# Steps of lead in a hand-scheduled attention loop: an even rate for the projections, one more empty piece ahead of some products, and maxima that end one step sooner

## The chip, the cores and the metric

The kernel runs on one core of a Trainium2 chip. The core has five engines that run side by side: TensorE (PE in the profile, with its weight loads as PEld), VectorE (DVE), ScalarE (ACT), GpSimd (POOL) and SyncE (SP), which issues most of the DMA. The metric is device time in microseconds (us); the number of a kernel is the median of its runs.

## What is computed

One transformer block with adaptive layer norm: causal attention with rotary position encoding, then a mixture of experts of which each token takes four of sixteen. There are 4 batches of 2048 tokens, 256 channels, 16 heads of 16 channels each. Cut to the part around the change:

```python
h = _layernorm(x) * (1 + ca) + sa
qkv = (h @ qkv_w + qkv_b)            # q, k: rotary
scores = einsum('bhqd,bhkd->bhqk', q, k) * scale   # causal mask
attn = softmax(scores)
x = x + ga * ((attn @ v) @ out_w + out_b)
h = _layernorm(x) * (1 + cb) + sb
x = x + gb * moe(h)                  # routing: top 4 of 16 experts, in 2 of 4 groups
```

## The kernel before, in words

Tokens are cut into 16 blocks of 512 (`NB`), four to a batch. The kernel has two stages: attention up to about 2780 us of the profiled execution, then the experts. The change lies in attention alone, though `send`, which carries a block over to the experts, is called in both stages.

**The main loop (L1204 to L1283).** A unit is one or two pairs of a block `n` and a group `g` of four heads: 16 units of one pair for batch 0, then 8 units of two pairs for each of the other batches, 40 in all (`units`, L927). A unit's steps go over its key tiles of 128: block `n` of a batch has 4 x (n % 4 + 1) of them, so that batch 0 makes 160 steps, each other batch 160, 640 in all. In a step TensorE puts the row maxima (product with `pick`, L1240) and the scores (L1247) into two PSUM tiles `st`, ScalarE takes exponentials into `e` (L1255), GpSimd masks the diagonal tiles (L1259), and one step later `weigh` (L1181) multiplies by the values into `po` (L1188). Of the last four key tiles of a block only 512, 384, 256 and 128 columns are computed.

**Maxima.** While a unit runs, the row maxima of the next one are made: `row_max` (L956) is a generator of pieces. Each computes scores into a PSUM tile `ps` (L968, from the same three buffers as `st`) that VectorE reduces (L978, L1001). Its last piece joins the parts into `negm` and splits them into three bf16 parts `mb` (L1014 to L1025). Then `max_rows` (L1028), after one empty piece, transposes `mb` on TensorE (`pmx`, L1034), and ScalarE copies the result to `mt`, which the next unit's first step needs. `draw` (L1219) spreads the pieces over the steps in proportion to `share` (L1211): 2 for a full step, less for a shortened one, with the last two steps left out. Two calls of `draw` in each step pull at most two pieces each.

**Background pieces.** Everything else in attention is a generator too, kept in one of six queues (`Background`, L65). A generator yields what its next piece needs: (a PSUM piece or not, VectorE time, GpSimd time). The `Budget` (L43) grants one PSUM piece for each step, since all of these products share one PSUM buffer (`wps`, one `"w"` tile), and a running account of VectorE and GpSimd time. `(0, 0, 0)` is an empty piece: it issues nothing and is there to put what follows later in the order. At a step's end (L1276 to L1282) the queues are served in turn: `over` (one piece, division by the row sum), `after_max` (one), `ends` (two, `finish`: output projection), `ahead` (projections), `after` (three: `send` and others).

**Projections (`prologue`, L814).** There are twelve, for the blocks of batches 1 to 3: load x, layer norm (`normalise`, L230), transposes (`pt`), then for each of four tiles of 128 tokens the products `pq` (L866) and `pv` (L879), rotary products on GpSimd (L893, L902), a transpose `ptq` (L907) of the rotated rows, copies on ScalarE and stores to DRAM. One is 48 pieces (`PIECES`, L922). How fast they are drawn is set by `marks` (L1168): for each unit that needs more projections than the one before, the step at which its loads are issued and the number of projections it needs. `due` (L1175) goes in straight lines between marks; a queue more than 8 pieces behind is pulled by force (L1279), else pieces are pulled as the budget allows, up to the due count.

**Send (`send`, L342).** For a block of the first twelve: load, layer norm, modulation on GpSimd, transposes, routing products (`lg`, L384), the ranks of `route` (L266: VectorE and GpSimd in turn), a count of the positions (`pk`, L402), and 16 scatters. Its argument `apart` is the number of empty pieces between an operation and one that takes its result on another engine: 1 in attention, 3 in the experts' stage. `normalise` has an argument `apart` of the same sense, 1 when the projections call it.

TensorE, ScalarE, VectorE and GpSimd run in the order in which the code issues (a manual schedule): a product whose input is late holds up all that stand behind it on TensorE.

Of the kernel before, what the change touches and what calls it, by code (L numbers as in the profile page):

```python
# [21 lines left out]
BT = 512  # L22
# [101 lines left out]
def adaln_attention_moe(  # L124
# [105 lines left out]
    def normalise(xb, pools, xn, apart=1):  # L230

        mv = pools.tile([P, 4, 2], F32, tag="mv", name="mv")
        for t in range(4):
            yield 0, 0.6, 0
            st = pools.tile([P, 6], F32, tag="bst", name="bst")
            nc.vector.bn_stats(st, xb[:, t, :])
            nc.vector.bn_aggr(mv[:, t, :], st)
        yield 0, 0.2, 1.0
        rs = pools.tile([P, 4], F32, tag="rs", name="rs")
        nc.vector.tensor_scalar_add(rs, mv[:, :, 1], EPS)  # L240
        nc.gpsimd.tensor_tensor(rs, rs, mhalf, ALU.pow)  # L241
        for _ in range(apart):
            yield 0, 0, 0
        for t in range(4):
            if t % 2 == 0:
                yield 0, 0.9, 0
            nc.vector.tensor_scalar(
                xn[:, t, :], xb[:, t, :], mv[:, t, 0:1], rs[:, t : t + 1], ALU.subtract, ALU.mult
            )
        return xn  # L250
# [320 lines left out]
    with ExitStack() as actx:  # L571
        acst = actx.enter_context(tc.tile_pool(name="acst", bufs=1))
        kvp = actx.enter_context(tc.tile_pool(name="kv", bufs=3))
        xp = actx.enter_context(tc.tile_pool(name="xa", bufs=1))
        tp = actx.enter_context(tc.tile_pool(name="ta", bufs=2))
# [4 lines left out]
        wps = actx.enter_context(tc.tile_pool(name="wps", bufs=1, space=PSUM))  # L580
# [233 lines left out]
        def prologue(n):  # L814

            b, qb = divmod(n, NQ)
            yield 0, 0, 0
            xb = xp.tile([P, 4, D], F32, tag="xp", name="xb")
            nc.sync.dma_start(xb, x[n * BT : (n + 1) * BT, :].rearrange("(t p) d -> p t d", p=P))
            for _ in range(3):  # L820
                yield 0, 0, 0
            xn = yield from normalise(xb, tp, xb)
            yield 1, 0, 0

            def evict(to, pt, k):
                nc.scalar.activation(
                    to,
                    pt,
                    AF.Identity,
                    bias=mod[:, k, b : b + 1],  # L830
                    scale=mod[:, 2 + k, b : b + 1],
                )

            hT = yield from transposed(xn, "hT", tp, wps, "w", evict)


            rest = None
            parts_ = [None]

            def high_low(t, pt):  # L840

                if t % 2 == 0:
                    parts_[0] = tuple(
                        tp.tile([P, 4, HB], FR, tag=name, name=name, bufs=1)
                        for name in ("high", "low")
                    )
                cols = slice(t % 2 * P, (t % 2 + 1) * P)
                nc.scalar.copy(parts_[0][0][:, :, cols], pt)
                whole = tp.tile([P, 4, P], F32, tag="whole", name="whole", bufs=1)
                nc.scalar.copy(whole, pt)  # L850
                return cols, whole

            def lower(cols, whole, high, low):
                nc.gpsimd.tensor_tensor(
                    low[:, :, cols], whole, high[:, :, cols].bitcast(F32), ALU.subtract
                )

            def halved(half, high, low):
                store(n, slice(half * HB, (half + 1) * HB), high, low, (nc.sync, nc.sync))

            for t in range(4):
                lT = [hT[:, k, t * P : (t + 1) * P] for k in range(2)]
                yield 1, 0.7, 0
                pq = wps.tile([P, BT], F32, tag="w", name="pq")
                for k in range(2):
                    nc.tensor.matmul(  # L866
                        pq, lhsT=lT[k], rhs=wqkv[:, k, : 2 * D], start=(k == 0), stop=(k == 1)
                    )
                qk = tp.tile([P, 2 * D], F32, tag="qk", name="qk", bufs=1)
                nc.vector.tensor_add(qk, pq, bqkv[:, : 2 * D])  # L870
                yield 0, 0, 1.3 if rest is not None else 0
                if rest is not None:
                    lower(*rest)
                    if t == 2:
                        halved(0, *rest[2:])
                yield 1, 0.4, 0
                pv = wps.tile([P, D], F32, tag="w", name="pv")
                for k in range(2):
                    nc.tensor.matmul(  # L879
                        pv, lhsT=lT[k], rhs=wqkv[:, k, 2 * D :], start=(k == 0), stop=(k == 1)  # L880
                    )
                nc.vector.tensor_add(
                    vh[:, :, t, :, 1:],
                    pv.rearrange("p (g h e) -> p g h e", g=NG, e=HD),
                    bqkv[:, 2 * D :].rearrange("p (g h e) -> p g h e", g=NG, e=HD),
                )
                parts = qk.rearrange("p (h e two) -> p h e two", e=HD // 2, two=2)
                full = [P, 2 * H, 2, HD // 2]
                prod = []
                for s in range(2):  # L890
                    yield 0, 0, 1.3
                    r_ = tp.tile(full, F32, tag=f"r{s}", name=f"r{s}", bufs=1)
                    nc.gpsimd.tensor_tensor(  # L893
                        r_,
                        parts[:, :, :, s].unsqueeze(2).to_broadcast(full),
                        rp[:, qb * 4 + t, s].unsqueeze(1).to_broadcast(full),
                        ALU.mult,
                    )
                    prod.append(r_.rearrange("p h a e -> p h (a e)"))
                xr = prod[0]  # L900
                yield 0, 0, 1.3
                nc.gpsimd.tensor_tensor(xr, xr, prod[1], ALU.add)  # L902
                yield 0, 0, 0
                yield 1, 0, 0
                pt = wps.tile([P, 4, P], F32, tag="w", name="ptq")
                for c_ in range(4):
                    nc.tensor.transpose(  # L907
                        pt[:, c_, :],
                        xr[:, 8 * c_ : 8 * c_ + 8, :].rearrange("p h d -> p (h d)"),
                        ident,  # L910
                    )
                cols, whole = high_low(t, pt)
                high, low = parts_[0]
                rest = (cols, whole, high, low)
            yield 0, 0, 1.3
            lower(*rest)
            yield 0, 0, 0
            halved(1, *rest[2:])
            nc.sync.dma_start(vd[n], va_new)


        PIECES = 48  # L922
        qts, kts, vas = {}, {}, {}


# [102 lines left out]
        def max_rows(n, g, mb):  # L1028

            yield 0, 0, 0  # L1030
            yield 1, 0, 0
            pm = wps.tile([P, 2, BT], BF, tag="w", name="pmx")
            for t in range(4):
                nc.tensor.transpose(pm[:, 0, t * P : (t + 1) * P], mb[:, t, :], idb)  # L1034
            mt = tp.tile([P, BT], BF, tag="mt", name="mt", bufs=3)
            nc.scalar.copy(mt, pm[:, 0, :])
            mts[n, g] = mt
# [31 lines left out]
        def finish(n):  # L1069
# [15 lines left out]
            xb = xp.tile([P, 4, D], F32, tag="xf", name="xb")  # L1085
# [27 lines left out]
                nc.vector.tensor_add(xb[:, halves[t2]], xb[:, halves[t2]], ps)  # L1113
            nc.sync.dma_start(x1d[n], xb.rearrange("p t d -> p (t d)"))
            if phase_of[n] is phases[0]:
                after.add(send(n, xp, tp, wps, "w"))
                finished.append(n)
                if len(finished) == len(phases[0].blocks):
                    after.add(find_tiles(phases[0]))

        budget = Budget()
        ahead, maxes, after_max, over, ends, after = (Background(budget) for _ in range(6))
# [38 lines left out]
        need, starts = [], [0]  # L1161
# [6 lines left out]
        marks = [(0, 0)]  # L1168
        for u in range(len(units)):

            step = starts[u - 1] - (starts[u - 1] - starts[u - 2]) // 3 if u > 1 else 0
            if need[u] > marks[-1][1]:
                marks.append((step, need[u]))

        def due(at):  # L1175
            for (a0, v0), (a1, v1) in zip(marks, marks[1:]):
                if at <= a1:
                    return int(-(-PIECES * (v0 + (v1 - v0) * (at - a0) / (a1 - a0)) // 1))
            return PIECES * marks[-1][1]

# [23 lines left out]
        for u, unit in enumerate(units):  # L1204
            steps_ = []
            for n, g in unit:
# [1 line left out]
                steps_ += [  # L1208
                    (n, g, k_, first_ + 4, max(0, k_ - first_) * P) for k_ in range(first_ + 4)
                ]  # L1210
            share = [2.0 - st_[4] / BT for st_ in steps_[: len(steps_) - 2]]  # L1211
            left = 0
            if u + 1 < len(units):
                left = max_pieces(units[u + 1])
# [75 lines left out]
    xp = ctx.enter_context(tc.tile_pool(name="xm", bufs=2))  # L1290
    tp = ctx.enter_context(tc.tile_pool(name="tm", bufs=2))
# [419 lines left out]
```

## Time and profile before

| | us |
|---|---|
| median of 3 runs | 3854.46 |
| lowest, highest | 3839.63, 3859.56 |
| the profiled execution | 3858.31 |
| its span, first to last instruction | 3856.1 |

| engine | busy us | share of the span | instructions |
|---|---|---|---|
| TensorE | 3230.1 | 84% | 19884 |
| VectorE | 2547.2 | 66% | 4534 |
| ScalarE | 1506.2 | 39% | 2140 |
| GpSimd | 1467.9 | 38% | 2170 |

The profile's page cuts the span into 40 slices of 96.4 us and gives each engine's busy share in tenths, with a row for the clock that TensorE was granted. A group is one line of the kernel on one engine: busy time and mean duration, then the engine's idle time just ahead of it, and what released it. A wait is named by the instruction that waited, then the one that it waited for. TensorE's busy time is modelled: its matmuls overlap. The mean granted clock over the span is 0.894.

### The profile page before, as it was taken

The numbers are of one execution on the slowest core, as the hardware profiler recorded it, in microseconds if no ns is written. First come the engines' busy times: TensorE is split into PE (matmuls) and PEld (weight loads), VectorE is DVE, ScalarE is ACT, GpSimd is POOL, SyncE is SP. The second block draws the span as 40 slices with busy tenths as digits, with TensorE's granted clock in tenths as the row PEclk, the third lists the DMA queues.
The fourth block names the chain that finished last, engine by engine and source line by source line (L and its number), as shares of the span: only waits on it lengthen the run. The fifth ranks groups of instructions, "written<-read, shape, count | busy, mean of one in ns | idle before, by whom it ended". The sixth has DMA issues, their size and how long they took to land. (4 is left out here: it accounts for less than half of the span.)

```text
span 3856.1 us, 55123 instructions
## 1 busy us (share of the span) xinstructions
PE 3230.1 (84%) x19884; PEld 1672.2 (43%) x20008; DVE 2547.2 (66%) x4534; ACT 1506.2 (39%) x2140; POOL 1467.9 (38%) x2170
## 2 busy tenths in 40 slices
PE   5388888888899989888898888899888898798893
PEld 3233333333334333333433333343366676575562
DVE  5256767766767767677767777677266576567774
ACT  1134444444454544444454444455522222121120
POOL 3213251522414253433425334311135555445554
PEclk8569988989899988988999999899988898899997
DMA  4444232321233322233333222311086666587763
GB/s 153 157 142 156 99 120 81 121 93 58 84 115 109 113 87 89 91 106 107 115 108 99 85 95 93 98 62 41 27 286 229 214 227 228 195 278 263 263 232 132
DMA packets 264635, 525.80 MB, mean 136 GB/s; under 512 B 26014, under 2 KB 133534, under 8 KB 264354
## 3 DMA queue, kind: packets, MB, share of 16 engines
q1 hardware_dynamic: 233890, 440.37, 33.6%
q0 software_dynamic: 26112, 73.44, 5.1%
q10 hardware_dynamic: 4352, 8.39, 0.6%
q8 instruction: 159, 2.61, 0.3%
q14 instruction: 122, 1.00, 0.1%
HBM read 336.47 MB, written 185.62 MB: 135 GB/s over the span
## 5 line engine op out<-in xcount | busy, mean ns | idle before, releaser
L1255 ACT ACTIVATE e<-st 128x1024 f32<-128x1024 f32 (+3 forms) x1280 | 1078.7, 895 | 1035.1 <-PE st L1247 978.7
L978 DVE TENSOR_REDUCE mparts<-ps 128x2 f32<-128x1024 f32 (+3 forms) x1152 | 1180.7, 1045 | 429.2 <-PE ps L968 367.1
L968 PE MATMUL ps<-kt,qt 64*128 64x512 f32 (+3 forms) x3328 | 619.5, 418 | 132.9 <-ACT e L1255 64.7
L1188 PE MATMUL po<-e,vg 128*32 128x512 f32 (+3 forms) x5120 | 671.7, 590 | 24.6 <-POOL e L1259 15.4
L968 PEld LDWEIGHTS ps<-kt,qt 64*128 64x128 f32 x3328 | 305.7, 205 | 730.9 <-ACT e L1255 443.4
L1259 POOL TENSOR_SCALAR_AFFINE_SELECT e<-e 128x256 f32<-128x256 f32 x512 | 206.8, 414 | 961.9 <-ACT e L1255 957.8
L1247 PE MATMUL st<-qt,kt 64*128 64x512 f32 (+3 forms) x2560 | 462.0, 441 | 0.0
L1358 PE MATMUL gu<-xT,wt 128*128 128x256 f32 x1728 | 416.5, 397 | 14.4 <-DVE xT L1347 8.3
L1461 POOL DMA_INDIRECT yd<-yt,to x288 | 282.8, 982 | 334.2 <-ACT yt L1457 140.3
L1240 PE MATMUL st<-mt,pick 32*128 32x512 bf16 (+3 forms) x2560 | 302.6, 372 | 94.8 <-DVE mparts L978 51.0
L1358 PEld LDWEIGHTS gu<-xT,wt 128*128 128x128 f32 x1728 | 333.4, 197 | 93.9 <-issue 36.2
L453 POOL DMA_INDIRECT xs<-row,rowx x256 | 249.0, 973 | 212.2 <-DVE row L444 157.4
L1001 DVE TENSOR_REDUCE mparts<-ps 128x8 f32<-128x1024 f32 x128 | 156.8, 1225 | 187.2 <-PE ps L968 170.3
L1247 PEld LDWEIGHTS st<-qt,kt 64*128 64x128 f32 x2560 | 205.3, 198 | 137.8 <-issue 125.9
L1240 PEld LDWEIGHTS <-pick 32*128 32x128 bf16 x2560 | 87.9, 91 | 311.1 <-issue 297.9
L1457 ACT ACTIVATE yt<-y,of 128x256 f32<-128x256 f32 x144 | 60.5, 471 | 396.5 <-DVE is L1437 140.9
L1188 PEld LDWEIGHTS po<-e,vg 128*32 128x32 f32 x5120 | 109.2, 112 | 182.9 <-issue 122.2
L1396 PE MATMUL y<-wt,ha 128*128 128x256 f32 x576 | 152.8, 404 | 30.5 <-issue 27.1
L893 POOL TENSOR_TENSOR r<-qk,rp 128x512 f32<-128x512 f32 x96 | 124.0, 1307 | 96.4 <-DVE qk L870 96.4
L241 POOL TENSOR_TENSOR rs<-rs,mhalf 128x4 f32<-128x4 f32 x32 | 34.9, 1090 | 265.1 <-DVE rs L240 209.1
L1396 PEld LDWEIGHTS y<-wt,ha 128*128 128x128 f32 x576 | 110.9, 202 | 55.1 <-issue 38.5
L1370 DVE TENSOR_TENSOR hb<-hb,gu 64x256 f32<-64x256 f32 x144 | 59.3, 412 | 105.6 <-ACT hb L1369 79.7
(227 smaller groups left out, 3639.8 us busy)
## 6 DMA issues: line engine op xcount, KB each, us to landing
wt<-in_w_all SPq DMA_DIRECT2D x144, 640.0 KB
kt<-kd SPq DMA_DIRECT2D x124, 512.0 KB
xt<-xs SPq DMA_DIRECT2D x144, 272.0 KB
qt<-qd SPq DMA_DIRECT2D x64, 512.0 KB
yg<-yd SPq DMA_DIRECT2D x16, 2048.0 KB
vg<-vd SPq DMA_DIRECT2D x124, 168.0 KB
xb<-in_x SPq DMA_DIRECT2D x32, 512.0 KB
qd<-high SPq DMA_DIRECT2D x96, 128.0 KB
```

What stands on the lines that cost most here:

```text
L453: s_ = nc.gpsimd.indirect_dma_start(out=ph.xs[:, :], out_offset=bass.IndirectOffsetOnAxis(ap=rowx[:, n, t, j : j + 1], axis=0), in_=row[:, ...
L968: nc.tensor.matmul(ps[:, half, to : to + width], lhsT=qt[rows, q, t * P : (t + 1) * P], rhs=kt[rows, q, key : key + width], start=start, s ...
L978: nc.vector.tensor_reduce(to, ps[:, :, :width], AX.X, ALU.max)
L1001: nc.vector.tensor_reduce(mine[:, :, :, 0], ps.rearrange("p h (t k) -> p h t k", k=P), AX.X, ALU.max,)
L1188: nc.tensor.matmul(po[32 * j : 32 * j + 32, off:], lhsT=va[:, k_, j * (HD + 1) : j * (HD + 1) + 32], rhs=es[j // 2][:, j % 2, off:], start ...
L1240: nc.tensor.matmul(sts[q][:, h_, off:], lhsT=pick[rows, :], rhs=mt[rows, off:], start=True, stop=False,)
L1247: nc.tensor.matmul(sts[q][:, h_, off:], lhsT=kt[rows, q, k_ * P : (k_ + 1) * P], rhs=qt[rows, q, off:], start=False, stop=True,)
L1255: nc.scalar.activation(es[q][:, :, off:], sts[q][:, :, off:], AF.Exp, scale=SCALE)
L1259: nc.gpsimd.affine_select(out=es[q][:, :, off : off + P], in_=es[q][:, :, off : off + P], compare_op=ALU.is_ge, fill=0.0, base=0, pattern= ...
L1358: nc.tensor.matmul(ps[:, c_ * TT : (c_ + 1) * TT], lhsT=wt[:, c_, k * 2 * I + cols : k * 2 * I + cols + P], rhs=xT[:, k, c_ * TT : (c_ + 1 ...
L1396: nc.tensor.matmul(pss[half][:, t, :], lhsT=ha[:, at_ : at_ + P], rhs=wt[:, half, 4 * I : 4 * I + D], start=(t == 0), stop=False, skip_gro ...
L1461: s_ = nc.gpsimd.indirect_dma_start(out=ph.yd[:, :], out_offset=bass.IndirectOffsetOnAxis(ap=to[:, t : t + 1], axis=0), in_=yt[:, t, :], i ...
```

## The change

Five edits, all in the order of issue; no operation is added or removed.

1. `marks` keeps only points at which the rate falls: a new mark removes earlier ones that lie on or below the line to it. The marks (step, projections) before are (0, 0), (139, 3), (214, 4), (294, 7), (374, 8), (454, 11), (534, 12); after it (0, 0), (454, 11), (534, 12).
2. `normalise` in `prologue` gets `apart` 2, and one empty piece more stands before each `ptq`; so `PIECES` is 53 (48 + 1 + 4).
3. `max_rows` has one empty piece more ahead of `pmx`.
4. `send` in attention gets `apart` 2: seven empty pieces more for each block.
5. `share` leaves out three steps at a unit's end, where the unit has more than four.

```diff
-            xn = yield from normalise(xb, tp, xb)
+            xn = yield from normalise(xb, tp, xb, 2)
...
                 nc.gpsimd.tensor_tensor(xr, xr, prod[1], ALU.add)
                 yield 0, 0, 0
+                yield 0, 0, 0
                 yield 1, 0, 0
                 pt = wps.tile([P, 4, P], F32, tag="w", name="ptq")
...
-        PIECES = 48
+        PIECES = 53
...
         def max_rows(n, g, mb):
 
             yield 0, 0, 0
+            yield 0, 0, 0
             yield 1, 0, 0
...
-                after.add(send(n, xp, tp, wps, "w"))
+                after.add(send(n, xp, tp, wps, "w", 2))
...
             if need[u] > marks[-1][1]:
+
+                while len(marks) > 1 and (need[u] - marks[-2][1]) * (
+                    marks[-1][0] - marks[-2][0]
+                ) >= (marks[-1][1] - marks[-2][1]) * (step - marks[-2][0]):
+                    marks.pop()
                 marks.append((step, need[u]))
...
-            share = [2.0 - st_[4] / BT for st_ in steps_[: len(steps_) - 2]]
+            share = [2.0 - st_[4] / BT for st_ in steps_[: len(steps_) - (3 if len(steps_) > 4 else 2)]]
```

## The prediction

> **What bounds the kernel now.** I read the page's slices first, then TensorE's work in stretches, then its groups and its waits inside attention, and last one unit's end in time.
>
> ```profile
> PE   5388888888899989888898888899888898798893
> PEclk8569988989899988988999999899988898899997
> ```
>
> The first row is TensorE's busy share, the second its granted clock. TensorE is at 80 to 90% from the third slice on, and no other engine comes near (page: DVE 66%, ACT 39%, POOL 38% of the span). So TensorE bounds attention, which runs from about 185 to 2780 us, and what can be won is its idle time and the clock below ten tenths. The MoE stage behind it is not touched.
>
> ```profile
> 185.30:811.60 626.30, 538.40 (x3473) 0.85 0.35 117
> 811.60:1120.40 308.80, 264.20 (x1801) 0.90 0.24 81
> 1120.40:1450.80 330.40, 296.96 (x2023) 0.93 0.33 111
> 1450.80:1781.80 331.00, 289.68 (x1969) 0.88 0.26 89
> 1781.80:2117.70 335.90, 298.20 (x2023) 0.93 0.34 114
> 2117.70:2442.20 324.50, 281.74 (x1971) 0.92 0.27 90
> 2539.10:2733.00 193.90, 177.12 (x1358) 1.00 0.13 46
> ```
>
> Columns: stretch, length, TensorE busy, granted clock, DMA share, GB/s. The cuts are the starts of the steps at which the planner's rate of projections changes (139, 214, 294, 374, 454, 534). The last row is steps 560 to 620, with no projections: 194/60 = 3.2 us a step at full clock. The third is 80 steps in which three projections are drawn, the fourth 80 steps with one, and so on in turn; there a step takes some 330/80 = 4.1 us. The clock loss up to 2442 us is the sum of (1 - clock) x length: 94 + 31 + 23 + 40 + 24 + 26 = 238 us.
>
> ```profile
> L968 PE MATMUL ps<-kt,qt 64*128 64x512 f32 (+3 forms) x3300 | 614.9, 417 | 131.7 <-ACT e L1255 64.7 <-DVE mparts L978 28.8 <-issue 12.7
> L1240 PE MATMUL st<-mt,pick 32*128 32x512 bf16 (+3 forms) x2560 | 302.6, 372 | 94.8 <-DVE mparts L978 51.0 <-ACT mt L1036 19.3 <-DVE mparts L1001 8.3
> L1034 PE MATMUL pmx<-idb,mb 128*128 128x128 bf16 x252 | 28.7, 246 | 24.8 <-DVE mb L1025 16.4 <-DVE run L418 3.2 <-DVE va L882 2.9
> L907 PE MATMUL ptq<-ident,r 128*128 128x128 f32 x192 | 35.1, 311 | 13.4 <-POOL r L902 8.6 <-POOL zeros L1146 2.5 <-ACT aT L1090 1.4
> L402 PE MATMUL pk<-chb,earlier 128*128 128x64 bf16 x12 | 2.4, 204 | 10.7 <-DVE chb L394 10.7
> L260 PE MATMUL pt<-ident,xb 128*128 128x128 f32 x96 | 19.3, 306 | 6.7 <-DVE xb L247 6.3 <-issue 0.4
> L260 PE MATMUL pt<-ident,row 128*128 128x128 f32 x96 | 16.4, 290 | 5.1 <-POOL row L368 5.1
> ```
>
> Groups of TensorE inside attention; the third field is idle time just before, with what ended it. The first two rows, 226.5 us, wait for a free PSUM buffer of the three that scores and maxima share. The other five are the products the change gives more lead: 24.8 + 13.4 + 10.7 + 6.7 + 5.1 = 60.7 us.
>
> ```profile
> PE st L1240 <- ACT mt L1036: 19.3, 15, 9.9
> PE pmx L1034 <- DVE mb L1025: 16.4, 9, 2.9
> PE po L1188 <- POOL e L1259: 15.4, 12, 2.5
> ```
>
> Waits inside attention: total, times, longest. One unit's end, in the same columns as the stretches above:
>
> ```profile
> 1798.00:1805.00 7.00, 4.24 (x42) 1.00 0.51 154
> 1805.00:1815.20 10.20, 9.43 (x51) 0.50 0.98 326
> ```
>
> TensorE is busy 61% of 7 us there, and the next 10.2 us run at half clock. An eight-matmul `po` product starting at 1813.20 us takes 1.93 us, at 1796.89 us 1.06 us: half of such a stretch is lost.
>
> **The change part by part.** It removes no operation and adds none: every matmul, reduction and copy is there as often as before, so all else is position. I counted positions by the planner's own rules (budgets, due counts, at most one PSUM piece a step) over the 640 steps, without times.
>
> *Maxima.* `share` leaves out the last three steps instead of two in units of more than four steps, so `mb` comes a step sooner; the empty piece in `max_rows` then leaves the `pmx` product where it was, last in its unit. In my count `mb` and `pmx` lie one step apart in 53 of 63 cases before and two in 62 after. Of the 24.8 us, by the timeline of its 64 products, 2.6 belong to the very first and about 3.5 to those drawn in block 0's units (four steps: `share` as before, product pulled by force). The rest, some 18 us, are waits of at most 2.9 us, against a step of 1.4 us or more of new lead: I take 18 as gone. The copy behind it (`ACT mt`, 19.3 us) stays: the product has not moved.
>
> *Send.* With `apart` 2, the pairs in one step (`rs` before rows 9 of 12, `gt` before `rk` 4, rows before transposes 3, `chb` before `pk` 2) all fall to none. Of 10.7 + 5.1 us I take 14. The seven more empty pieces a send cost nothing: nobody waits for a send before the MoE stage, and by the count the last one's scatters end at step 542 instead of 541. If that cover were gone, each step of delay would put 3 to 4 us on the end.
>
> *Projection.* Rotated rows and their `ptq` fall in one step 14 times of 48 before and 8 after, because `ahead` still catches up with its due count in bursts: 13.4 x 6/14 = 5.7 us. Normalised rows and their transpose: 6 of 12 to 3, 6.7/2 = 3.3 us.
>
> *Even rate.* Before, the marks ask for 1.04 pieces a step to step 139, then 0.64, 1.8, 0.6, 1.8, 0.6. After, four marks go: 11 x 53/454 = 1.28 pieces up to step 454, then 0.66. About 0.6 of a projection moves into batch 0, with its x load on SP and its q, k, v stores, past loads that its units need; these queues have room (DMA share 0.35 there, and no row above waits for a load). The stretches show what a projection costs where it goes: three each in 330.4 and 335.9 us, one each in 331.0 and 324.5, that is (666.3 - 655.5)/4 = 2.7 us for one, whether drawn fast or slowly. So evening them out is worth between -5 and +5 us; I take 0. Only if the clock follows the bunching is it more, and the heavy stretches have the better clock (0.93, 0.93 against 0.88, 0.92).
>
> Direct sum: 18 + 14 + 5.7 + 3.3 = 41 us off.
>
> *Clock.* The Trainium skill, TensorE: Matmul & The Clock Gate, section Why this matters for your kernels, says half clock comes from idle gaps over about 3 us. No wait named here is that long (2.9 at most), so by the rule the change wins nothing from the clock. The trace says otherwise: half clock follows a stretch with 39% idle in pieces. Shared out by idle time (the third field summed over all groups in attention, 328 us), the 60.7 us answer for 238 x 60.7/328 = 44 us of clock loss, the 41 us removed for 30; since other gaps in those stretches stay, I take half, 15. Bounds 0 and 30.
>
> *What it costs.* (a) Some 42 pieces of maxima a unit go into 32.5 instead of 34.25 parts of `share`, 5.4% denser. Waits of TensorE on `mparts` are 28.8 + 51.0 + 8.3 = 88 us; by proportion +5, at twice that +10. (b) One more step at a unit's end has no maxima to fill it, so `po` reaches POOL's masks sooner: 15.4 us of such waits, half as much again is +8; nearest row the other way is the last unit, without maxima, which hardly waits: 0. (c) My count has seven `pmx` pulled by force at a unit's start instead of three (block 0's units), each behind another piece in the only `wps` buffer: 4 x 1 = 4 us. Taken: 5 + 8 + 4 = 17; bounds 4 and 25.
>
> Sum: 41 + 15 - 17 = 39 us. The profiled execution took 3858.3 us with a span of 3856.1, four above the median of 3854.5; on the median that is 3815 us.
>
> **The rivals.**
>
> *More (3765 us, 0.10).* The clock is freed beyond its share: 60 direct and 30 clock give 90. For it: half clock lasts longer than the gaps that bring it on. Against: the PSUM waits, four times larger, bring it on too.
>
> *No change (3852 us, 0.22).* What `pmx`, `pk` and `ptq` no longer wait, `ps` and `st` wait instead, on the three shared PSUM buffers: with three quarters of 41 + 15 given back, 14 stay, less (b) and (c), 12: 2 us. For it: 226.5 us of idle time is there, nearly four times the five rows. A sister of it: the change doesn't do what it says for projections, since the due count (53 instead of 48) draws the added empty pieces in the same burst; the 8 of 48 left show this in part.
>
> *Slower (3892 us, 0.23).* The cut of `share` starves unit ends. Their last steps have 128 to 384 of 512 columns; without maxima TensorE has little to do there and the busy share falls under the 61% seen above, so that a stretch at half clock follows. One of 6.8 us loses 3.4 us, with 0.5 of idle time 3.9. There are 35 such ends; 20 of them give 78 - 41 = 37 us on top. It decides from 41/3.9, some 11 ends. For it: the two rows at 1798 us are just such an end. Against: in the last 60 steps, whose units end the same way, the clock is 1.00.
>
> **How the numbers follow.** Likeliest, 0.45: 3815, its own range 3787 to 3838 (41 + 30 - 4 = 67 off, or 41 + 0 - 25 = 16). With the rivals at 0.10, 0.22 and 0.23, 3770 to 3885 leaves out most of More and half of Slower, some 0.18. A difference under 0.5% (19 us) is about what a measurement of this kernel can't tell from none. Faster by more than that: 0.45 + 0.10 = 0.55; within: 0.22; slower: 0.23.
>
> **What would show it.** Right: idle before `pmx` from 24.8 to under 8 us, before `pk` and the row transposes from 15.8 to under 3, before `ptq` to about 8, the clock up by 0.01 in the stretches, `ps` and `st` idle within 10 us of 226.5. Wrong: `ps` and `st` idle up by 40 (No change), or `po` idle doubled and unit ends followed by half clock (Slower). I am also wrong if the even rate does something of its own, seen as batch 0 longer than before (up to step 160, about 898 us) by more than later stretches are shorter.

## The result, and the profile after

| | before, us | after, us |
|---|---|---|
| median (4 runs each) | 3850.86 | 3902.07 |
| lowest, highest | 3839.63, 3859.56 | 3896.65, 3911.54 |
| the profiled execution | 3858.31 | 3896.65 |
| its span | 3856.1 | 3894.9 |

The ratio is 1.0139 (95% interval 1.011 to 1.0169): slower by 1.4%, outside the range and on the other side of it. Lines behind L819 have moved by one to seven (L968 is L969, L1240 is L1247, L1255 is L1262).

The page's slices of after, TensorE's busy share and its clock:

```profile
PE   5378888887879889888988898898978898798893
...
PEclk8579989899889989898989898899988898899997
```

The clock is no worse than before, the busy share is a little lower. TensorE's stretches of after, cut at the starts of the same steps as those before (stretch, length, busy, clock, DMA share, GB/s):

```profile
185.90:814.20 628.30, 527.35 (x3466) 0.89 0.36 118
814.20:1144.10 329.90, 274.20 (x1869) 0.90 0.28 95
1144.10:1467.60 323.50, 287.06 (x1994) 0.94 0.29 100
1467.60:1796.00 328.40, 288.70 (x1996) 0.92 0.29 99
1796.00:2141.00 345.00, 292.68 (x2001) 0.92 0.29 97
2141.00:2471.60 330.60, 285.89 (x1944) 0.88 0.25 84
2574.20:2774.70 200.50, 179.53 (x1360) 0.99 0.13 44
```

The first six rows are steps 0 to 534: 2285.7 us, against 2256.9 before, and TensorE busy 1955.9 against 1969.2. So 28.8 us more length is 13.3 us less work time and 42.1 us more idle time. The last row, steps without projections, went from 193.9 to 200.5 us: only the edits of the maxima reach it. Batch 0 (step 0 to 160) took 713 us against 712: no harm from the even rate shows there.

The groups of TensorE in attention, after (idle time just before, and what ended it, in the last fields):

```profile
L1195 PE MATMUL po<-e,vg 128*32 128x512 f32 (+3 forms) x5120 | 676.6, 585 | 43.3 <-POOL e L1266 33.3 <-POOL between L463 5.3 <-issue 4.3
L969 PE MATMUL ps<-kt,qt 64*128 64x512 f32 (+3 forms) x3300 | 604.2, 411 | 163.1 <-ACT e L1262 77.9 <-DVE mparts L979 27.7 <-issue 25.6
...
L1247 PE MATMUL st<-mt,pick 32*128 32x512 bf16 (+3 forms) x2560 | 304.3, 369 | 126.1 <-DVE mparts L979 77.0 <-ACT mt L1038 20.7 <-DVE mparts L1002 9.6
...
L992 PE MATMUL ps<-mask,idb 128*128 128x512 bf16 x132 | 53.9, 417 | 24.9 <-ACT e L1262 14.8 <-issue 5.3 <-DVE mparts L979 3.4
...
L908 PE MATMUL ptq<-ident,r 128*128 128x128 f32 x192 | 33.7, 301 | 5.3 <-POOL r L902 4.0 <-POOL zeros L1148 1.3
L1036 PE MATMUL pmx<-idb,mb 128*128 128x128 bf16 x252 | 28.1, 241 | 5.3 <-DVE mb L1026 2.7 <-DVE atok L1060 1.6 <-ACT hT L826 0.9
...
L260 PE MATMUL pt<-ident,row 128*128 128x128 f32 x96 | 15.7, 286 | 0.0
...
L402 PE MATMUL pk<-chb,earlier 128*128 128x64 bf16 x12 | 2.5, 207 | 0.9 <-DVE chb L394 0.9
```

Two groups of before that the prediction did not show:

```profile
L1188 PE MATMUL po<-e,vg 128*32 128x512 f32 (+3 forms) x5120 | 671.7, 590 | 24.6 <-POOL e L1259 15.4 <-POOL between L463 5.5 <-issue 3.4
...
L991 PE MATMUL ps<-mask,idb 128*128 128x512 bf16 x129 | 55.4, 434 | 13.7 <-ACT e L1255 5.2 <-issue 4.6 <-DVE mparts L978 2.3
```

The five products that were to get lead idle 5.3 + 5.3 + 0.9 + 0.0 and 7.6 (`pt` of `xb`) = 19.1 us instead of 60.7. That is 41.6 us gained, as forecast. Other products took it back and more: `ps` 131.7 to 163.1, `st` 94.8 to 126.1, `po` 24.6 to 43.3, the mask product of L992 13.7 to 24.9; together 92.6 us. (In both traces some 120 of the 252 records of the mask product are missing, 129 and 132 are there; their time shows as idle before the `ps` behind them, 24.7 and 29.8 us in the 128-column form, and only the difference counts. Of the experiments below, e1 to e7 and e10 have all records.)

### The profile page after: what moved, and what is told of

Read it like the earlier page. It is cut to its first block, busy times and chain, and to the rows that moved or that the text cites. A ratio compares the mean times of both kernels' runs of the same rounds, so it can differ in the third digit from the quotient of the medians.

```text
span 3894.9 us, 55079 instructions
## 1 busy us (share of the span) xinstructions
PE 3221.2 (83%) x19887; PEld 1667.5 (43%) x20008; DVE 2558.6 (66%) x4534; ACT 1502.7 (39%) x2140; POOL 1467.0 (38%) x2170
## 5 line engine op out<-in xcount | busy, mean ns | idle before, releaser
L1262 ACT ACTIVATE e<-st 128x1024 f32<-128x1024 f32 (+3 forms) x1280 | 1079.0, 895 | 1105.1 <-PE st L1254 999.0
L969 PE MATMUL ps<-kt,qt 64*128 64x512 f32 (+3 forms) x3328 | 608.8, 412 | 164.2 <-ACT e L1262 77.9
L1195 PE MATMUL po<-e,vg 128*32 128x512 f32 (+3 forms) x5120 | 676.6, 585 | 43.3 <-POOL e L1266 33.3
L969 PEld LDWEIGHTS ps<-kt,qt 64*128 64x128 f32 x3328 | 299.2, 201 | 737.4 <-ACT e L1262 403.0
L1247 PE MATMUL st<-mt,pick 32*128 32x512 bf16 (+3 forms) x2560 | 304.3, 369 | 126.1 <-DVE mparts L979 77.0
L1247 PEld LDWEIGHTS <-pick 32*128 32x128 bf16 x2560 | 88.4, 91 | 358.2 <-issue 345.6
L854 POOL TENSOR_TENSOR low<-whole,high 128x512 fp32r<-128x512 f32 x48 | 61.3, 1276 | 312.1 <-ACT whole L850 300.4
L893 POOL TENSOR_TENSOR r<-qk,rp 128x512 f32<-128x512 f32 x96 | 123.9, 1306 | 76.1 <-DVE qk L870 76.1
```

The lines of the kernel that those rows point to most:

```text
L969: nc.tensor.matmul(ps[:, half, to : to + width], lhsT=qt[rows, q, t * P : (t + 1) * P], rhs=kt[rows, q, key : key + width], start=start, s ...
L1195: nc.tensor.matmul(po[32 * j : 32 * j + 32, off:], lhsT=va[:, k_, j * (HD + 1) : j * (HD + 1) + 32], rhs=es[j // 2][:, j % 2, off:], start ...
L1247: nc.tensor.matmul(sts[q][:, h_, off:], lhsT=pick[rows, :], rhs=mt[rows, off:], start=True, stop=False,)
L1262: nc.scalar.activation(es[q][:, :, off:], sts[q][:, :, off:], AF.Exp, scale=SCALE)
```

## The experiments

The kernels ran on five chips: on four of them the kernel before takes 3753 to 3759 us, called A below, and on the fifth 3848 us, called B. The chip of the first comparison is not on record; its 3851 us and its traces (below) are like those of B, and it is counted with B. Each ratio is to the kernel before on the same chip; it is the ratio on record, which can differ from the quotient of the two medians by up to 0.2 points. The ranges in us that the first expectations give are counted from 3851, so only their distance from it can be compared. In these expectations and below, T is the starved unit end (the rival "Slower"), D is the time of VectorE's full-width reductions, R blames the even rate or the empty pieces, P is the order of the three shared PSUM buffers whatever VectorE's speed, and Q is the case of two maxima drawn ahead of `weigh` in one step.

**Which edit costs.** Each of the next six leaves out or adds edits.

```diff
# e1_cut: before with edit 5 alone
-            share = [... steps_[: len(steps_) - 2]]
+            share = [... steps_[: len(steps_) - (3 if len(steps_) > 4 else 2)]]
# e10_cut4: the same with 4 in place of 3
# e3_cut_max: e1_cut and edit 3 (one more empty piece in max_rows)
# e2_no_cut: after without edit 5
# e4_even: before with edit 1 alone, PIECES 48
# e7_lead: edits 1, 2 and 4; share and max_rows as before
```

> The kernel before with one edit of the five: share leaves out three steps. Theory D (VectorE's rate): a full-width maximum takes VectorE 1.22 us, three in a step 3.66 us, more than the step has to offer, so the denser drawing lengthens full steps by some 0.1 us each; the trace of after shows 6.7 us more in the 60 steps that have nothing else to do, so 640 steps give 50 to 65 us: 3900 to 3915 us. Theory T (starved unit ends: masks awaited, half clock behind them): also 40 to 60 us more, but in the last steps of units and not in full ones. Theory R (the even rate or the empty pieces did it): no change, 3840 to 3860 us.

> The changed kernel with share put back to two steps; even rate and all empty pieces stay. Theories D and T: the loss is gone, and of the 41 us of shorter waits at pmx, pk, ptq and the transposes some part shows: 3815 to 3850 us; pmx waits again in part, since mb is no longer a step sooner. Theory R: 3890 to 3905 us as in the changed kernel.

> The kernel before with the cut of share and the empty piece in max_rows, the two edits that deal with maxima. D and T: like the cut alone, 3895 to 3915 us, the piece itself worth no more than 10 us either way. R: 3840 to 3860 us.

> The kernel before with the even rate alone (marks of falling rate, PIECES still 48). R: 30 to 50 us slower, 3880 to 3900 us. D and T: within 15 us of before, 3835 to 3865 us, since a projection cost the same where it was drawn fast and slowly.

> The kernel before with the even rate and the empty pieces of projections and send, and neither edit on maxima. D: the best of them, 0.5 to 1.0% faster than before, since the piece in max_rows, which costs 0.57% beside the cut, is gone too. If that piece helps without the cut, no better than 0.4%.

> The kernel before with share leaving out four steps in units of more than four: a dose test. Maxima 12% denser than before instead of 5.4%. D: full steps lengthen further, the loss is 2 to 3%. P or T alone, with one more step without maxima at each unit's end: about twice the 0.91% of the cut by three, 1.8%, and then in the last steps of units.

| kernel (all on A) | median, us | ratio to before, 95% |
|---|---|---|
| e1_cut | 3798.35 | 1.0091 (1.0064 to 1.0117) |
| e3_cut_max | 3814.10 | 1.0148 (1.0118 to 1.0178) |
| e10_cut4 | 3883.33 | 1.0342 (1.0305 to 1.0379) |
| e4_even | 3744.97 | 0.9961 (0.9942 to 0.9979) |
| e7_lead | 3711.40 | 0.9871 (0.9843 to 0.9899) |
| e2_no_cut | 3740.02 | 0.9954 (0.9928 to 0.9979) |

The edits fall into two camps. Even rate and lead for projections and send gain 1.3% (e7_lead, the best of the complete versions). Both edits of the maxima cost: the cut alone 0.9%, a cut of four 3.4%, the empty piece 0.4% behind the cut (3814.10/3798.35) and 0.8% on top of lead (e2_no_cut against e7_lead, on two chips). The cut's 40 us lie at the lower end of what T said (40 to 60) and below what D said (50 to 65). R falls: e4_even and e7_lead are faster than before. The size of the cut of four, 3.4%, was foreseen by none (D said 2 to 3%, T and P about 1.8%), and the piece costs more than the 10 us that were allowed to it.

Where the cut's loss goes is read from e4_even and e1_cut, on one chip. They differ by the cut and by the even rate, which touches no maximum. The groups of their `ps` products by width, first e4_even:

```profile
L991 PE MATMUL ps<-mask,idb 128*128 128x512 bf16 x252 | 82.8, 413 | 7.7 <-ACT e L1260 3.9 <-DVE mparts L978 1.2
...
L968 PE MATMUL ps<-kt,qt 64*128 64x384 f32 x252 | 55.9, 440 | 1.0 <-DVE mparts L1001 0.8
```

Then e1_cut:

```profile
L991 PE MATMUL ps<-mask,idb 128*128 128x512 bf16 x252 | 83.1, 414 | 21.1 <-ACT e L1255 16.2 <-DVE mparts L978 2.9
...
L968 PE MATMUL ps<-kt,qt 64*128 64x384 f32 x252 | 55.6, 438 | 15.0 <-ACT e L1255 14.2 <-DVE mparts L1001 0.8
```

The maxima of the diagonal tiles (384 columns, and the masked ones) now wait for ScalarE. A step of e1_cut on TensorE (start, duration, idle before) shows why:

```profile
1324.04 0.73 PE L1247 MATMUL st<-qt,kt 64*128 64x512 f32 x4
1324.60 0.28 PE L968 MATMUL ps<-kt,qt 64*128 64x256 f32 x2
1325.71 0.44 PE L968 MATMUL ps<-kt,qt 64*128 64x384 f32 x2 [0.83 <-ACT e L1255]
1326.08 1.07 PE L1188 MATMUL po<-e,vg 128*32 128x512 f32 x8
```

Two maxima stand between `st` and `po`. `st` holds two of the three shared buffers and the first maximum the third, so the second waits until ScalarE has read a tile of `st` (the wait shown is 0.83 us), and `po` stands behind it. In e4_even the same pair lies on both sides of `po`, and in a short step:

```profile
1095.45 0.28 PE L968 MATMUL ps<-kt,qt 64*128 64x256 f32 x2
1095.67 0.85 PE L1193 MATMUL po<-e,vg 128*32 128x384 f32 x8
1096.45 0.45 PE L968 MATMUL ps<-kt,qt 64*128 64x384 f32 x2
```

The next table counts, over attention, the pairs of maxima that stand ahead of `po`. Their number follows from the order of issue and is the same in every kernel without the cut (before, e2, e4, e5, e7) and in every kernel with a cut of three (after, e1, e3, e6, e16, e17, e19); the other columns are us of idle time before the second maximum:

| pair | number without the cut | with it | before | e4_even | after | e1_cut |
|---|---|---|---|---|---|---|
| 512 + 512 | 72 | 66 | 42.5 | 37.8 | 39.6 | 35.1 |
| 512 + masked | 6 | 29 | 3.9 | 2.9 | 19.8 | 13.9 |
| 256 + 384 | none | 17 | none | none | 14.0 | 13.8 |
| 384 + 512 | none | 9 | none | none | 6.5 | 7.3 |
| 128 + 256 | 4 | 5 | 2.9 | 2.6 | 4.3 | 3.6 |
| together | 82 | 126 | 49.3 | 43.2 | 84.1 | 73.7 |

So the cut makes 44 pairs more and 30 to 35 us more of stalls, some 0.7 us for each. (Some 20 pairs in which the masked maximum comes first never waited, and are left out. Of the 35 us between before and after, 12 are waits that end by "issue" and not by ScalarE.) In e1_cut the 30 us stand beside 40 us (3798.35 - 3744.97 = 53, of which the missing even rate is 14). Added to it are `po` waits for the masks (25.2 to 31.3 us).

The dose test does not fit the pairs alone. e10_cut4 has 159 of them with 81.2 us of stalls, 38 more than e4_even, but it costs some 130 us. Its mean granted clock in attention is 0.901, against 0.911 in e4_even. What makes up the rest of its loss was not separated.

T falls by the unit ends. From before to after, the last four steps of all units of more than four steps went from 169.7, 122.5, 82.4 and 107.8 us to 135.2, 95.2, 101.0 and 95.2, 56 us shorter in all, and TensorE's idle time in them from 76 to 65 us, while the full steps (512 columns) in front of them went from 1782.7 to 1889.8.

**Is it VectorE?** Half-width reductions leave half of the keys of full stretches out of the row maximum.

```diff
# e5_half: before with
-                    nc.vector.tensor_reduce(to, ps[:, :, :width], AX.X, ALU.max)
+                    nc.vector.tensor_reduce(to, ps[:, :, : width // 2], AX.X, ALU.max)
# e6_half_cut_max: the same edit in e3_cut_max
```

> The kernel before with VectorE's maximum over the first half of each stretch of keys only (the other half of the scores is computed on TensorE but left out of the row maximum): 1.22 us becomes about 0.7 us. A base for the next run. D: VectorE sets the length of full steps that carry three maxima, so a good part of the idle time before ps and st goes: 40 to 120 us faster. A theory P (the three shared PSUM buffers and their order, whatever VectorE's speed): within 20 us of before.

> The same half-width maxima, with the two edits on maxima (share cut by three steps, the empty piece in max_rows), which cost 1.48% with full-width maxima. D: against the run with half-width maxima the loss falls to under 0.5%, since three maxima in a step now take VectorE 2.1 us. P and T: the loss stays at 1 to 1.5%.

Both on A: 3585.28 us, ratio 0.9541 (0.9513 to 0.957), and 3656.29, 0.9734 (0.9704 to 0.9763). Halving most of VectorE's reductions (1.23 us becomes 0.69) is worth 4.6% to the kernel as a whole, some 170 us: more than D said, and far outside the 20 us of P. But cut and piece cost 3656.29/3585.28 = 1.0198 here, no less than the 1.0148 at full width. So D, as the cause of this loss, falls as well: the loss doesn't shrink with the reduction. The pairs fit that: e5 has 82 of them with 58.9 us, e6 has 126 with 89.7, so again 44 more and 31 us, and what their second maximum waits for is ScalarE.

**Is it the second maximum ahead of `weigh`?** The limit keeps to one there, and leaves the rest to the second call of `draw`.

```diff
-            def draw(upto):
+            def draw(upto, most=2):
...
-                n = min(int(want - drawn), 1 if want - drawn < 3 else 2)
+                n = min(int(want - drawn), 1 if want - drawn < 3 else most)
...
-                draw(sum(share[:s_]) + (share[s_] / 2 if s_ < len(share) else 0))
+                draw(sum(share[:s_]) + (share[s_] / 2 if s_ < len(share) else 0), 1)
# e11_after_one, e20_after_one_again: in after
# e12_before_one: in before;  e13_lead_one: in e7_lead
# e14_lead_cut_one: in e7_lead with edit 5
# e15_cut_one: in e1_cut;  e18_half_cut_max_one: in e6_half_cut_max
```

> The changed kernel, all five edits, with one limit: the draw ahead of weigh pulls at most one maximum, never two (the second draw may still pull two). Theory Q (two maxima ahead of weigh): the second one asks for a PSUM buffer that ScalarE's exponential of the same step still reads, and weigh stands behind it; after has 77 such full steps from step 160 on, 23 of them with two maxima ahead and none behind, at some 0.6 to 1.6 us each; so the limit takes off 60 to 100 us and the changed kernel becomes faster than before: ratio 0.985 to 0.999. Theory D or T (density, or starved ends, whatever the order): the density is as it was, so the ratio stays at 1.01 or above.

> The kernel before with the same limit of one maximum ahead of weigh. Q: 55 such full steps from step 160 on, all with a third maximum behind, at about 0.4 to 0.6 us each: 20 to 35 us faster, ratio 0.991 to 0.995. D or T: no change, 0.997 to 1.003.

> Even rate and empty pieces of projections and send (0.9871 without the limit), with the limit of one maximum ahead of weigh. Q: another 25 to 40 us off, ratio 0.976 to 0.981. D or T: 0.985 to 0.990.

> The same with share cut by three steps and no empty piece in max_rows, so that mb and pmx both come a step sooner than before. Q: the cut itself costs little once no two maxima stand ahead of weigh, and pmx no longer makes the units of batch 0 wait for its copy: ratio 0.972 to 0.985. D or T: the cut costs its 0.9% again, 0.985 to 0.997.

> The cut of share by three steps with the limit of one maximum ahead of weigh, and nothing else of the change. Q (the cut costs because it puts more steps with two maxima ahead of weigh, 131 full ones instead of 99): the loss of 0.91% is gone, 0.996 to 1.002. D (density as such): 1.007 to 1.011 as without the limit.

> Half-width maxima (the other half of the keys left out of the row maximum), cut of share, empty piece in max_rows, and the limit of one maximum ahead of weigh. Q: the order of issue and not VectorE's time makes the loss, so the limit takes it away here too: from 0.9734 to 0.955 to 0.963, near the 0.9541 of half-width maxima alone. D: no change from 0.9734.

> The changed kernel with at most one maximum ahead of weigh, again. Q (the order ahead of weigh makes the loss): 1.5 to 2.5% below its twin. A theory C (the limit does nothing, and the chip made the earlier difference): within 0.4% of its twin.

| kernel | chip | median, us | ratio to before, 95% |
|---|---|---|---|
| e11_after_one | A | 3720.74 | 0.9909 (0.9886 to 0.9931) |
| e20_after_one_again | A | 3719.76 | 0.9907 (0.9879 to 0.9934) |
| e12_before_one | A | 3758.00 | 1.0009 (0.9993 to 1.0024) |
| e13_lead_one | A | 3712.55 | 0.9894 (0.9870 to 0.9919) |
| e14_lead_cut_one | A | 3715.37 | 0.9899 (0.9875 to 0.9924) |
| e15_cut_one | B | 3919.65 | 1.0187 (1.0158 to 1.0215) |
| e18_half_cut_max_one | B | 3718.58 | 0.9667 (0.9643 to 0.9690) |

With the limit no such pair is left. What TensorE waits for in e20_after_one_again (total, times, longest):

```profile
PE st L1247 <- DVE mparts L979: 68.0, 106, 3.0
...
PE st L1247 <- DVE mparts L1002: 26.3, 40, 1.8
...
PE ps L969 <- ACT e L1262: 20.1, 68, 0.6
```

The same waits in the whole change without the limit, on the same chip (e19_after_third, below):

```profile
PE ps L969 <- ACT e L1262: 71.7, 133, 1.1
...
PE st L1247 <- DVE mparts L979: 61.0, 76, 4.5
...
PE st L1247 <- DVE mparts L1002: 8.6, 15, 1.8
```

So 52 us of waits for ScalarE go, 25 us of waits for VectorE come, and the time falls from 3749.26 to 3719.76, 0.8%: 30 us, about the stalls of the pairs that the cut made. With lead and with the limit the cut costs nothing that can be measured (e14 against e13, on one chip). Before and e7_lead have 82 pairs too, most of them 512 + 512, and there the limit wins nothing (e12, e13): in e13 against e7_lead 34 us of waits for ScalarE go and 22 us for VectorE come.

This supports Q for the pairs that the cut adds, on A and beside lead, and no further. Of Q's forecasts for these seven kernels only e11's came true. e12, e13 and e14 gained less than it said, and there the ranges of D or T were met; e18 missed by 0.4 points; e20 lies 0.8% below its twin instead of 1.5 to 2.5%. e15_cut_one speaks against Q as the whole cause: it has no such pair left, and on B it still costs 1.9%. e18 and e6 stand on different chips, and can't be set against each other for the limit. The whole change with the limit was not run on B, where the change costs 1.4 to 1.65%.

**The same program on several chips.** e11 was 0.9% faster than before, though the change that it starts from had been 1.4% slower in the first comparison. So the whole change was run again, unchanged, on two chips, and e7_lead with the cut on one.

> Even rate, empty pieces of projections and send, and the cut, without the limit and without the piece in max_rows. Q: the cut's loss of about 0.9% or more comes on top of 0.9871, so 0.996 to 1.006, while the same with the limit took 0.9899. If the limit did nothing there: 0.987 to 0.992.

> The changed kernel as it is, for a comparison on one chip with its parts. 1.009 to 1.017 if the result carries over to this chip; Q then puts the worth of the limit at the difference to 0.9909.

> The changed kernel once more, beside its twin with the limit on one chip. Q and D: 1.006 to 1.017, whichever chip it is.

| kernel | chip | median, us | ratio to before, 95% |
|---|---|---|---|
| e16_lead_cut (edits 1, 2, 4, 5) | B | 3877.98 | 1.0074 (1.0053 to 1.0094) |
| e17_after_again (after) | B | 3912.02 | 1.0165 (1.0138 to 1.0193) |
| e19_after_third (after) | A | 3749.26 | 0.9986 (0.9966 to 1.0006) |

The change costs 1.65% on B and nothing that can be measured on A, so the forecast of e19 (1.006 to 1.017) was missed; e16 lies just above Q's range. The empty piece alone is 0.9% on B (3912.02/3877.98). What sets B apart in the traces is a kind of wait for which no releaser is found. In before, then in after, inside attention (total, times, longest):

```profile
DVE mparts L978 <- remote: 32.2, 9, 6.2
...
ACT e L1255 <- remote: 24.4, 7, 7.5
...
DVE mparts L1001 <- remote: 6.7, 1, 6.7
```

```profile
ACT e L1262 <- remote: 60.4, 12, 11.8
DVE mparts L979 <- remote: 59.8, 10, 11.7
```

"Remote" stands for another core or a queue that the trace doesn't know, and there is no other core here. In each of them ScalarE or VectorE waits on a product of TensorE that by the trace ended over 1.5 us earlier. Before has 63.3 us of them, after 124.5 (with two small rows), e17 123.9, e16 90.1, e15 113.1, e18 106.4; the fourteen traces from A have none. The experts' stage, which the change doesn't touch, shows the same: 1077 us with 90 us of such waits in before, 1020 us with none in e4_even. One place of after, step 382 (13.1 us; 3.0 in e19_after_third), in its timeline (start, duration, idle before):

```profile
1828.27 0.96 DVE L979 TENSOR_REDUCE mparts<-ps 128x2 f32<-128x768 f32 x1 [3.63 <-remote]
...
1829.28 0.39 PE L1247 MATMUL st<-mt,pick 32*128 32x512 bf16 x2 [2.40 <-issue]
...
1833.31 1.23 DVE L1002 TENSOR_REDUCE mparts<-ps 128x8 f32<-128x1024 f32 x1 [4.08 <-remote]
1834.59 0.47 PE L969 MATMUL ps<-kt,qt 64*128 64x128 f32 x2 [4.01 <-DVE mparts L1002]
...
1836.95 1.94 ACT L1262 ACTIVATE e<-st 128x1024 f32<-128x1024 f32 x2 [11.78 <-remote]
```

All engines but GpSimd stand still in turn, and TensorE's next stall, 4.01 us, is put down to VectorE, though VectorE only passed a "remote" wait on. That stretch and the one behind it (length, busy of PE, PEld, DVE, ACT, POOL, then the clock):

```profile
1824.00:1838.00 14.00, 6.52 (x42) 2.21 (x34) 3.93 (x7) 2.22 (x4) 9.02 (x18) 0.71 0.60 207
1838.00:1846.00 8.00, 7.97 (x44) 3.52 (x48) 4.18 (x10) 4.94 (x6) 0.00 (x0) 0.65 0.02 5
```

The stall costs more than its own length, since half clock follows. Between after (B) and e19 (A), the same program, attention differs by 94 us; 36 steps that differ by over 1 us make up more than all of it (129.9), and the median durations of instructions are equal. In after and e17 these waits fall largely on the same places of the program: ten of the twelve steps that have them in after have them in e17. So they seem to belong to places in the instruction stream, on a chip like B.

## Why the prediction was wrong

*Lead: right.* Forecast 41 us of direct idle time, measured 41.6: `pmx` 24.8 to 5.3 (forecast under 8), `pk` and row transposes 15.8 to 0.9 (under 3), `ptq` 13.4 to 5.3 (about 8). That the sum agrees to 1 us is partly luck, since `pt` of `xb` did not fall. And `pmx`, nearly half of it, was bought by the two edits that cost: in e7_lead, without them, it still idles 21.1 us. Lead of the other products and even rate together are worth 1.3% (e7_lead, 42 us between the medians).

*Even rate: near.* Taken at 0 between -5 and +5; e4_even shows 0.39% off, 15 us, by an edit that touches nothing else. The bounds were too tight.

*Clock: right size, cause not separated.* Forecast 15. The loss as (1 - clock) x length over steps 0 to 534 went from 238 to 215 us, and the work time in them by 13 us. No run shows which edit did it. "No wait named here is that long (2.9 at most)" was misread: the row of `mt` shown there has one of 9.9 us, before the first product of attention, and the trace of before has gaps of 3.3 to 6.0 us inside attention.

*Costs: the failed step.* The prediction put the denser drawing of the maxima, its term (a), at +5 to +10 us by scaling the waits for `mparts`, and held `ps` and `st` within 10 us of 226.5. They rose by 62.7 us to 289.2, the mask product by 11.2 more. (a) was wrong in its form. `draw` deals in whole pieces: a few per cent denser means 44 steps more with two maxima ahead of `weigh`, 30 to 35 us of stalls. And it was taken on the wrong row: I scaled the waits on VectorE's `mparts` (88 us), while these stalls are mostly waits on ScalarE's `e`, whose 64.7 us stood in the first row that I showed. The 5.4% hold for units of two pairs; in batch 0's units of one pair the parts of `share` fall from 11.75, 19.75 and 27.75 to 10, 18 and 26, 7 to 18% denser, and 19 of the 44 added pairs lie there. (b), +8 for the masks, went the right way and came to 6 (e1_cut against e4_even) to 19 (after against before).

Two more terms were put at nothing. The empty piece in `max_rows` was only to leave `pmx` where it was; it costs 0.4 to 0.9% wherever it was added. And the "remote" waits had no term: between before and after they rise by 61 us. ScalarE and VectorE often have them at once; counted once, they cover 52 us of before and 91 of after, and TensorE's own gaps that overlap them come to 31 and 54 us.

How the distance of 90 us, from 39 faster to 51 slower, divides among these three is not shown. The stalls of the pairs are read from the traces and, on A, tested by the limit; on B, e15_cut_one has none of them and still loses.

*The rivals.* "Slower" said 3892, near the 3902, but by a mechanism that did not occur: unit ends grew shorter. "No change" had the mechanism, PSUM waits in place of the waits removed, and its sign to watch for (`ps` and `st` up by 40; measured 31.4 + 31.3 = 62.7), but not that they can take back more than was won. On A its result, no change, is what was measured.

*The parts.* On A: lead and even rate -1.3%, the piece in `max_rows` +0.8%, the cut +0.3%, which is hardly clear of noise (e7_lead, e2_no_cut, e19_after_third in turn), in all -0.1%. The cut costs 0.9% without lead, so the parts don't simply add. What B has beyond A is 1.5 to 1.8 points, 57 to 69 us. The "remote" waits fit as its cause, with the half clock behind them, but this was not tried: no edit here takes such a wait away by itself.

*Open.* What the "remote" waits are, and why the changed order meets twice as many. Why cut and limit without lead cost 1.9% on B: there is no run of it on A, and the trace has 50 us more of "remote" waits than before. Why the empty piece in `max_rows` costs what it does: it moves a product that nothing seemed to wait for, and TensorE's idle time in attention is about 260 us with it (e2_no_cut) and without it (e7_lead). The best version, e7_lead, was measured on A alone.

## What to carry to other kernels

More lead for a product that stalls its queue takes away about what its idle row says (here 41.6 us of 60.7). Lead that is bought by drawing other work sooner is paid in whole pieces: count the steps in which one piece more lands between a producer and its consumer on the same engine, ask which buffer that piece needs and who frees it, and price each; don't scale a sum of waits by a few per cent. Run each edit alone, and before a change of one or two per cent is believed, run the same pair on a second chip.

## What the runs showed of the hardware

The clock that TensorE is granted was 1.0 or 0.5, and nothing between, in the single records. In attention of before every record lasts a multiple of 3.41 us. In the 3.41 us ahead of a fall to half, TensorE was busy under 62% in 53 of 68 cases and under 73% in 63; of the 469 such windows after which full clock stayed, 7 were under 62%. Ahead of each of the 68 returns to full clock it was busy at least 89.5%. So low busy share goes with the fall, but no single bound parts all cases. The Trainium skill, TensorE: Matmul & The Clock Gate, section Why this matters for your kernels, speaks of gaps over about 3 us; only 5 of these 68 falls had a gap of 3 us or more in or reaching into that window, and the measurement decides. Eight `po` matmuls took 1.06 us at full clock and 1.93 at half.

The same program differs between chips beyond its own scatter: before by 2.4% (3757 us on A, 3848 on B), the change's ratio by 1.5 to 1.8 points, and on B most of the longest stalls of the change sit at the same places of the program in two traces.
